# Attention block on one core: the product with v and the fp32 projections in two column halves, softmax sums by VectorE group adds, and the last output projection block by block

## The chip, the cores and the metric

One core of a Trainium2 chip runs one program. The metric is the device time of that program in microseconds (us). Engines are called by the profile's names: PE is TensorE (PEld its weight loads), DVE is VectorE, ACT is ScalarE, POOL is GpSimd, SP is SyncE.

## The reference

Input x is (4, 512, 48, 48) in fp32: 4 images, 512 channels, 2304 positions. 8 heads of 64 channels.

```python
hn = _group_norm(x, gn_scale, gn_bias)                       # 32 groups
qkv = einsum('oc,bchw->bohw', qkv_w, hn) + qkv_b             # fp32
q, k, v = qkv.reshape(b, 3, heads, 64, t).astype(float16)
w = softmax(einsum('bhct,bhcs->bhts', q * scale, k * scale))  # over s
a = einsum('bhts,bhcs->bhct', w, v).astype(float32)
return x + einsum('oc,bchw->bohw', proj_w, a) + proj_b
```

## The kernel before

The program is `fast_path`; the other path, `general_path`, runs only if a flag computed at the end of `fast_path` says that a softmax sum left its allowed range, and it does not run here. Heads are taken in pairs: a pair g (0 to 15) is two heads of one image, 128 channels; four pairs make an image. Positions stand in 18 key tiles of 128 and in 5 query blocks, four of 512 and one of 256.

**Attention.** The work of a pair is a list of 81 units (`units_of`): for a block of 512 queries one unit for each of the 18 key tiles, for the block of 256 one unit for two key tiles. `scores` (line 747) multiplies k and q of both heads, each on its own 64 rows of the array (line 755), into a PSUM tile of 128x1024, and ACT takes the exponential of that into fp16 (line 763). `values` (line 766) multiplies the exponentials with v, one product for each head (line 777). The stationary operand there has 65 columns: 64 of v and one of ones, so that row 64 of the result is the softmax sum. After a block's last unit `finish` (line 787) copies both results out of PSUM (line 792), sends the sums through small DMAs to take reciprocals across partitions (line 798) and to spread them again (line 804), and DVE multiplies (line 808).

**Projections.** q, k and v come from fp32 products of the normalised image with `wqkv`, accumulated over four channel chunks: `qk_items` (line 624, 40 items a pair, 32 of 512 columns and 8 of 256) and `v_items` (line 670, 72 items of 512 columns an image). An item is one product. Each fp32 product stands in the trace as two matmul records. `proj_items` (line 697) is the output projection of one block: 16 items, each with two fp32r products (high and low part of the weights, line 714); POOL first casts the four pairs' results to fp32r (line 704), and DVE adds bias and x (line 723).

**Order.** The main loop takes units two at a time, called a burst here: first the scores of this burst, then the values of the burst before, then `fill`, which issues as many items from the list `beside[g]` as the share of pair g's units that are done. There are 648 bursts, 40 or 41 a pair. A scheduler orders each engine's instructions when the program is built, so an instruction whose buffer isn't free lets later ones of its engine past. What `beside` holds: the q and k projections of a pair two pairs ahead, from pair 2 of an image the load and norm of the next image (`turn`) and then its v projection, in pair 3 of an image the q and k projections of the next image's first two pairs. The output projection of image b stands beside image b+1, in its pairs 0 and 1; that of image 2 stands in pairs 14 and 15, and that of image 3 after all attention:

```python
late = b == B - 1
beside[g + (2 + j // 3 if late else j // 4)] += proj_items(b - 1, j)
...
for j in range(NQ):
    for _, run in proj_items(B - 1, j):
        run()
```

The results of a pair (`atts[g]`) have 5 buffers, so pair 13 writes into the buffer that pair 8 had, which is free when image 2's output projection has read it. Ahead of the loop image 0 is normalised and its v and first two pairs of q and k are projected.

Of the kernel before, what the change touches and what calls it, by code (L numbers as in the profile page):

```python
# [30 lines left out]
SCALE = float(np.float16(1.0 / math.sqrt(math.sqrt(D))))  # L31
LAG = 2


# [431 lines left out]
def fast_path(  # L466
# [48 lines left out]
    nc.sync.dma_start(bproj, proj_b)  # L515
    brow = const.tile([1, C], F32, name="brow")
    nc.sync.dma_start(
# [41 lines left out]
    ones = const.tile([P, 1], F32, name="ones")  # L559
    nc.gpsimd.memset(ones, 1.0)  # L560

    bqk = const.tile([P, 2 * NC], F32, name="bqk")
# [47 lines left out]
    def qk_items(g):  # L610
# [8 lines left out]
        def one(part, j, c, pw):  # L619
            o, n = QBLOCKS[j]  # L620
            if c == 0:
                pw[0] = ps_w.tile([P, QB], F32, tag="pw", name=f"pqk_{g}_{part}_{j}")
            w0 = part * C + pr * P
            nc.tensor.matmul(  # L624
                pw[0][:, :n],
                wqkv[:, c, w0 : w0 + P],
                hn[b][c][:, o : o + n],
                start=(c == 0),
                stop=(c == NC - 1),
            )  # L630
# [27 lines left out]
    def v_items(b):  # L658
        items = []

        def new():
            for pr in range(NPAIR):
                t = vpool.tile([P, NT, 2, D + 1], F16, tag="v", name=f"v_{b}_{pr}")
                nc.gpsimd.memset(t[:, :, :, D : D + 1], 1.0)
                vv[b * NPAIR + pr] = t

        def one(i, c, pw):
            if c == 0:
                pw[0] = ps_w.tile([P, QB], F32, tag="pw", name=f"pv_{b}_{i}")
            nc.tensor.matmul(  # L670
                pw[0],
                hn[b][c][:, bass.ts(i, P)],
                wqkv[:, c, 2 * C :],
                start=(c == 0),
                stop=(c == NC - 1),
            )
            if c == NC - 1:
                for pr in range(NPAIR):
                    cols = bass.ts(pr, P)
                    nc.vector.tensor_tensor(  # L680
                        vv[b * NPAIR + pr][:, i, :, 0:D],
                        pw[0][:, cols].rearrange("p (h d) -> p h d", d=D),
                        bv[:, cols].rearrange("p (h d) -> p h d", d=D),
                        ALU.add,
                    )
# [50 lines left out]

    av, pts = {}, {}

    def units_of(g):
        found = []  # L740
        for j, (o, n) in enumerate(QBLOCKS):
            per = QB // n
            for i in range(0, NT, per):
                found.append((g, j, list(range(i, i + per))))
        return found

    def scores(u):
# [16 lines left out]
        pts[g, j, keys[0]] = pt  # L764

    def values(u):
        g, j, keys = u
        o, n = QBLOCKS[j]
        if keys[0] == 0:
            if j == 0:  # L770
                atts[g] = apool.tile([P, T], F16, tag="att", name=f"att_{g}")
            for h in range(2):
                av[h] = ps_av.tile([D + 1, QB], F32, tag=f"av{h}", name=f"av{h}_{g}_{j}")
        pt = pts.pop((g, j, keys[0]))
        for h in range(2):
            for a, i in enumerate(keys):
                nc.tensor.matmul(  # L777
                    av[h][:, :n],
                    vv[g][:, i, h, :],
                    pt[:, h, a * n : (a + 1) * n],  # L780
                    start=(i == 0),
                    stop=(i == NT - 1),
                )
        if keys[-1] == NT - 1:
            finish(g, j)

    def finish(g, j):
        o, n = QBLOCKS[j]
        per = n // P
        avx = work.tile([P, 2, QB], F32, tag="avx", name=f"avx_{g}_{j}")  # L790
        for h in range(2):
            nc.vector.tensor_copy(avx[0 : D + 1, h, :n], av[h][:, :n])  # L792
        first = 2 * o // P
        sm = sums[:, g, first : first + 2 * per].rearrange("p (h i) -> p h i", h=2)
        for h in range(2):
            nc.sync.dma_start(sm[:, h, :], avx[D : D + 1, h, :n])
        inv = small.tile([P, 2, QB // P], F32, tag="inv", name=f"inv_{g}_{j}")
# [4 lines left out]
        )  # L802
        ib = work.tile([D, 2, QB], F32, tag="ib", name=f"ib_{g}_{j}")
        nc.sync.dma_start(  # L804
            ib[:, :, :n], row[:, :n].unsqueeze(0).to_broadcast((D, 2, n))
        )
        for h in range(2):
            nc.vector.tensor_tensor(  # L808
                atts[g][h * D : (h + 1) * D, o : o + n],
                avx[0:D, h, :n],  # L810
                ib[:, h, :n],
                ALU.mult,
            )

    beside = {g: [] for g in range(NG)}
    for b in range(B):
        g = b * NPAIR  # L820
        for pr in (2, 3):
            beside[g + pr - 2] += qk_items(g + pr)
        if b > 0:
            for j in range(NQ):
                late = b == B - 1
                beside[g + (2 + j // 3 if late else j // 4)] += proj_items(b - 1, j)
        if b + 1 < B:

            def turn(b=b):
                hn[b + 1] = load_x(b + 1, (nc.gpsimd, nc.gpsimd))  # L830
                norm(b + 1)

            beside[g + 2].insert(0, (0.0, turn))
            vs = v_items(b + 1)
            beside[g + 2] += [(45.0, lambda: None)] + vs[:55]
            beside[g + 3] += vs[55:]
            for pr in (0, 1):
                beside[g + 3] += qk_items(g + NPAIR + pr)

# [7 lines left out]
    stream = [u for g in range(NG) for u in units_of(g)]  # L847
    last_of = {}
    for n, u in enumerate(stream):
        last_of[u[0]] = n  # L850
    per_pair = len(stream) // NG
    state = {"g": 0, "done": 0.0}

    def fill(n):

        g = stream[n][0]
        todo = beside[g]
        if state["g"] != g:
            state.update(g=g, done=0.0)
        if "total" not in state or state.get("of") != g:  # L860
            state.update(total=sum(w for w, _ in todo), of=g)
        place = n - g * per_pair + 1
        share = state["total"] * place / (per_pair - 2)
        while todo and state["done"] <= share:
            w, run = todo.pop(0)
            run()
            state["done"] += w

    waiting = []
    for n in range(0, len(stream), 2):  # L870
        burst = stream[n : n + 2]
        for u in burst:
            g = u[0]
            if g > 0 and u[1] == 0 and u[2][0] == 0:
                while beside[g - 1]:
# [6 lines left out]
    for u in waiting:  # L882
        values(u)
    for j in range(NQ):
        for _, run in proj_items(B - 1, j):
            run()


    flat = sums.rearrange("p g n -> p (g n)")
    low = small.tile([P, NG * 2 * NT], F32, tag="low", bufs=1, name="low")  # L890
    nc.vector.tensor_scalar(low, flat, SUM_MIN, None, ALU.is_ge)
    both = small.tile([P, NG * 2 * NT], F32, tag="both", bufs=1, name="both")
    nc.vector.scalar_tensor_tensor(both, flat, SUM_MAX, low, ALU.is_le, ALU.mult)
    good = small.tile([P, 1], F32, tag="good", bufs=1, name="good")
    nc.vector.tensor_reduce(good, both, AX.X, ALU.add)
    pf = ps_w.tile([1, 1], F32, tag="pw", name="count")
    nc.tensor.matmul(pf, good, ones, start=True, stop=True)
    nc.vector.tensor_scalar(flag, pf, float(B * HEADS * T) - 0.5, None, ALU.is_lt)
# [53 lines left out]
```

## Time and profile before

| | before |
|---|---|
| median of 3 runs | 2035.42 us (2035.2 to 2035.8) |
| the profiled execution | 2034.5 us, its span 2032.8 us |
| mean granted TensorE clock | 0.989 |
| busy share of the span | PE 96%, ACT 61%, DVE 26%, POOL 3% |

The span runs from the first to the last instruction of the profiled execution; 1.7 us of its time lie around the span. Busy is the time in which an engine has an instruction running. A matmul's record is longer than its place in the stream, since matmuls are pipelined: the distance between two starts is what one costs.

### The profile page before, as it was taken

Reading aid. Unit: us, or ns where it says so; the run is one execution under the profiler, and the core shown is the slowest. Engines: PE = TensorE matmul, PEld = TensorE weight load, DVE = VectorE, ACT = ScalarE, POOL = GpSimd, SP = SyncE. Lnnn points to the kernel's source line nnn. Section 1 sums busy time; section 2 is a strip of 40 time slices with the busy share of each in tenths; the row PEclk is TensorE's granted clock in tenths of the full one; section 3 lists DMA queues with packets and bytes.
Section 4 is the critical chain, followed back from the end, with each engine's and each line's share of the span. In section 5 each row is a group of like instructions: output and inputs, shape, how many; then the busy total and the mean of one; then the engine's idle time right before and its main releaser. Section 6 shows DMA issues by size and latency. Waiting matters only on the chain. (4 is left out here: it accounts for less than half of the span.)

```text
span 2032.8 us, 21633 instructions
## 1 busy us (share of the span) xinstructions
PE 1948.3 (96%) x8274; PEld 852.8 (42%) x8274; DVE 520.3 (26%) x1101; ACT 1243.3 (61%) x1297; POOL 66.1 (3%) x134
## 2 busy tenths in 40 slices
PE   3999999899999999899999999989999999999997
PEld 1444444234444553434344454433444434453335
DVE  5221222422222222522222222252222221131113
ACT  0007878755556667675555657775555788549990
POOL 0000000000000000100000010000000000010001
PEclk9999999899999999899999999989999999999999
DMA  5000002100000230400000041130000000141105
GB/s 191 0 0 6 16 9 87 31 11 9 11 6 14 76 101 11 135 11 11 8 6 14 6 130 53 49 98 11 9 6 11 14 11 14 42 137 22 27 24 176
DMA packets 83237, 81.80 MB, mean 40 GB/s; under 512 B 50356, under 2 KB 56500, under 8 KB 83124
## 3 DMA queue, kind: packets, MB, share of 16 engines
q1 hardware_dynamic: 77508, 60.67, 11.1%
q0 software_dynamic: 3456, 14.16, 1.8%
q10 hardware_dynamic: 2160, 5.51, 0.8%
q8 instruction: 67, 1.10, 0.2%
q14 instruction: 46, 0.38, 0.1%
HBM read 60.83 MB, written 19.17 MB: 39 GB/s over the span
## 5 line engine op out<-in xcount | busy, mean ns | idle before, releaser
L763 ACT ACTIVATE p<-ps 128x1024 f16<-128x1024 f32 x1296 | 1242.0, 1038 | 719.9 <-PE ps L755 668.7
L777 PE MATMUL av<-p,v 128*65 128x512 f16 (+1 forms) x2880 | 730.7, 368 | 25.9 <-DVE avx L792 25.9
L624 PE MATMUL pqk<-x,wqkv 128*128 128x512 f32 (+1 forms) x1280 | 556.1, 552 | 4.1 <-DVE x L598 4.1
L755 PE MATMUL ps<-q,k 64*128 64x512 f16 (+1 forms) x2880 | 435.5, 362 | 8.4 <-ACT p L763 6.0
L777 PEld LDWEIGHTS <-v 128*65 128x65 f16 x2880 | 262.9, 111 | 387.4 <-issue 294.6
L755 PEld LDWEIGHTS <-k 64*128 64x128 f16 x2880 | 125.3, 94 | 453.5 <-issue 448.9
L624 PEld LDWEIGHTS pqk<-x,wqkv 128*128 128x128 f32 x1280 | 241.6, 191 | 151.1 <-issue 98.9
L670 PE MATMUL pv<-wqkv,x 128*128 128x512 f32 x576 | 263.7, 593 | 0.0
L808 DVE TENSOR_TENSOR att<-avx,ib 64x512 f16<-64x512 f32 (+1 forms) x160 | 101.3, 633 | 295.2 <-DMA ib<-row 291.7
L670 PEld LDWEIGHTS pv<-wqkv,x 128*128 128x128 f32 x576 | 107.8, 190 | 102.6 <-issue 92.7
L792 DVE COPY avx<-av 65x512 f32<-65x512 f32 (+1 forms) x160 | 94.4, 628 | 214.2 <-PE av L777 213.0
L714 PE MATMUL pr<-a,whi 128*128 128x512 f32 (+1 forms) x320 | 131.5, 416 | 11.8 <-POOL a L704 7.1
L680 DVE TENSOR_TENSOR v<-pv,bv 128x128 f16<-128x128 f32 x288 | 63.8, 286 | 221.0 <-PE pv L670 220.9
L714 PE MATMUL pr<-a,wlo 128*128 128x512 f32 (+1 forms) x320 | 120.1, 380 | 0.0
L633 DVE TENSOR_SCALAR k<-pqk,bqk 128x512 f16<-128x512 f32 (+1 forms) x80 | 55.7, 696 | 247.3 <-PE pqk L624 247.1
L633 DVE TENSOR_SCALAR q<-pqk,bqk 128x512 f16<-128x512 f32 (+1 forms) x80 | 55.7, 696 | 237.6 <-PE pqk L624 237.3
L723 DVE SCALAR_TENSOR_TENSOR x<-pr,bproj,x 128x512 f32<-128x512 f32 (+1 forms) x80 | 55.5, 695 | 110.2 <-PE pr L714 80.8
L704 POOL CAST a<-att 128x512 fp32r<-128x512 f16 (+1 forms) x80 | 43.6, 582 | 1218.3 <-PE pr L714 553.9
L714 PEld LDWEIGHTS pr<-a,whi 128*128 128x128 f32 x320 | 61.2, 191 | 37.7 <-POOL a L704 18.8
L714 PEld LDWEIGHTS pr<-a,wlo 128*128 128x128 f32 x320 | 61.2, 191 | 11.0 <-issue 1.8
L798 DVE RECIPROCAL inv<-sums 128x8 f32<-128x8 f32 (+1 forms) x80 | 15.8, 197 | 149.2 <-DMA sums<-avx 146.9
L573 DVE BATCH_NORM_STATS2 st<-x 128x6 f32<-128x384 f32 x96 | 46.1, 537 | 8.7 <-DMA x<-x_dram 8.7
(36 smaller groups left out, 72.2 us busy)
## 6 DMA issues: line engine op xcount, KB each, us to landing
x<-x_dram SPq DMA_DIRECT2D x64, 256.0 KB, 2.9
ib<-row SPq DMA_DIRECT2D x64, 256.0 KB, 3.5
out_dram<-x SPq DMA_DIRECT2D x64, 256.0 KB, 2.4
x<-x_dram POOLq DMA_DIRECT2D x24, 576.0 KB, 7.1
wqkv<-qkv_wT_dram ACTq DMA_DIRECT2D x3, 1024.0 KB, 10.9
x<-x_dram SPq DMA_DIRECT2D x4, 576.0 KB, 7.6
x<-x_dram ACTq DMA_DIRECT2D x4, 576.0 KB, 9.0
sums<-avx SPq DMA_DIRECT2D x128, 2.0 KB, 2.0
```

The lines of the kernel that those rows point to most:

```text
L573: nc.vector.bn_stats(st[:, j, :], hn[b][c][:, bass.ts(j, SB)])
L624: nc.tensor.matmul(pw[0][:, :n], wqkv[:, c, w0 : w0 + P], hn[b][c][:, o : o + n], start=(c == 0), stop=(c == NC - 1),)
L633: nc.vector.tensor_scalar(qk[g][part][:, o : o + n], pw[0][:, :n], SCALE, bqk[:, col : col + 1], ALU.mult, ALU.add,)
L670: nc.tensor.matmul(pw[0], hn[b][c][:, bass.ts(i, P)], wqkv[:, c, 2 * C :], start=(c == 0), stop=(c == NC - 1),)
L680: nc.vector.tensor_tensor(vv[b * NPAIR + pr][:, i, :, 0:D], pw[0][:, cols].rearrange("p (h d) -> p h d", d=D), bv[:, cols].rearrange("p (h ...
L714: nc.tensor.matmul(pw[0][:, :n], w[:, c, bass.ts(m, P)], at[0][:, c, :n], start=(c == 0 and i == 0), stop=(c == NC - 1 and i == 1),)
L723: nc.vector.scalar_tensor_tensor(xt, pw[0][:, :n], bproj[:, m : m + 1], xt, ALU.add, ALU.add)
L755: nc.tensor.matmul(ps[:, h, a * n : (a + 1) * n], k[rows, bass.ts(i, P)], q[rows, o : o + n], start=True, stop=True,)
L763: nc.scalar.activation(pt, ps, AF.Exp)
L777: nc.tensor.matmul(av[h][:, :n], vv[g][:, i, h, :], pt[:, h, a * n : (a + 1) * n], start=(i == 0), stop=(i == NT - 1),)
L792: nc.vector.tensor_copy(avx[0 : D + 1, h, :n], av[h][:, :n])
L808: nc.vector.tensor_tensor(atts[g][h * D : (h + 1) * D, o : o + n], avx[0:D, h, :n], ib[:, h, :n], ALU.mult,)
```

## The change

`values` gives each head's product 64 columns of v instead of 65. Head 0 writes partitions 0 to 63 of one PSUM tile and head 1 partitions 64 to 127, so each uses one half of the array's columns, and the loops are turned so that the halves alternate. The column of ones goes away. Instead DVE adds the exponentials of up to six units of a block into an fp16 tile of 128x1024 (in `scores`, so one add for each unit but the first of a group), and one product with a 128x64 matrix of ones for each head and group gives the sums, again in two column halves, into a PSUM tile `sl`.

The fp32 projections of q, k and v are split likewise: each product with 128 output columns becomes two with 64. The output projection stays whole.

`finish` copies one 128x512 tile of results and one of sums, spreads the reciprocals with two DMAs instead of one, and the multiply is one instruction on POOL instead of two on DVE. v stands in one tile an image, and its bias is added by one DVE instruction a tile instead of four.

The order changes in the last six pairs: pair 11 no longer projects q and k of pair 13, which moves to pair 12 (and 14 to 13, 15 to 14). The output projection of image 2 stands beside pairs 12 (four blocks) and 13 (one block). That of image 3 stands beside pair 15, each block released 12 units after its attention ended; what is left over runs after the loop.

```diff
-    vpool = ctx.enter_context(tc.tile_pool(name="vpool", bufs=6))
+    vpool = ctx.enter_context(tc.tile_pool(name="vpool", bufs=2))
-    ppool = ctx.enter_context(tc.tile_pool(name="ppool", bufs=4))
+    ppool = ctx.enter_context(tc.tile_pool(name="ppool", bufs=6))
+    ps_l = ctx.enter_context(tc.tile_pool(name="ps_l", bufs=1, space=PSUM))
...
-            nc.tensor.matmul(
-                pw[0][:, :n],
-                wqkv[:, c, w0 : w0 + P],
-                hn[b][c][:, o : o + n],
+            for lo in (0, D):
+                nc.tensor.matmul(
+                    pw[0][lo : lo + D, :n],
+                    wqkv[:, c, w0 + lo : w0 + lo + D],
+                    hn[b][c][:, o : o + n],
...
-            nc.tensor.matmul(
-                pw[0],
-                hn[b][c][:, bass.ts(i, P)],
-                wqkv[:, c, 2 * C :],
+            for lo in (0, D):
+                nc.tensor.matmul(
+                    pw[0][lo : lo + D, :],
+                    hn[b][c][:, i * P + lo : i * P + lo + D],
+                    wqkv[:, c, 2 * C :],
...
-                for pr in range(NPAIR):
...
+                nc.vector.tensor_tensor(vv[b][:, i, :], pw[0], bv, ALU.add)
...
         nc.scalar.activation(pt, ps, AF.Exp)
         pts[g, j, keys[0]] = pt
 
+        m = keys[0] // len(keys)
+        key = (g, j, m // SUMMED)
+        if m % SUMMED == 0:
+            acc[key] = pt
+            return
+        before = acc[key]
+        if m % SUMMED == 1:
+            acc[key] = work.tile(
+                [P, 2, QB], F16, tag="acc", name=f"acc_{g}_{j}_{m // SUMMED}"
+            )
+        nc.vector.tensor_tensor(acc[key], before, pt, ALU.add)
...
-        for h in range(2):
-            for a, i in enumerate(keys):
+        for a, i in enumerate(keys):
+            for h in range(2):
+                lo = h * D
                 nc.tensor.matmul(
-                    av[h][:, :n],
-                    vv[g][:, i, h, :],
+                    av[0][lo : lo + D, :n],
+                    vv[b][:, i, pr * P + lo : pr * P + lo + D],
                     pt[:, h, a * n : (a + 1) * n],
...
+        if m % SUMMED == SUMMED - 1 or keys[-1] == NT - 1:
+            t = acc.pop((g, j, m // SUMMED))
+            for a in range(per):
+                for h in range(2):
+                    lo = h * D
+                    nc.tensor.matmul(
+                        sl[0][lo : lo + D, :n],
+                        ones16,
+                        t[:, h, a * n : (a + 1) * n],
...
-        for h in range(2):
-            nc.vector.tensor_copy(avx[0 : D + 1, h, :n], av[h][:, :n])
+        nc.vector.tensor_copy(avx[:, :n], av[0][:, :n])
+        slx = work.tile([P, QB], F32, tag="slx", bufs=1, name=f"slx_{g}_{j}")
+        nc.vector.tensor_copy(slx[:, :n], sl[0][:, :n])
...
+        for h in range(2):
+            nc.sync.dma_start(
+                ib[h * D : (h + 1) * D, :n], row[h : h + 1, :n].to_broadcast((D, n))
+            )
+        nc.gpsimd.tensor_tensor(
+            atts[g][:, o : o + n], avx[:, :n], ib[:, :n], ALU.mult
         )
-        for h in range(2):
-            nc.vector.tensor_tensor(
-                atts[g][h * D : (h + 1) * D, o : o + n],
...
+            put(g, qk_items(g + 2))
+            put(g + 1, qk_items(g + 3))
             vs = v_items(b + 1)
+            put(g + 2, [(0.0, turn), (45.0, lambda: None)] + vs[:55])
+            put(g + 3, vs[55:] + qk_items(g + 4))
+            if b + 2 < B:
+                put(g + 3, qk_items(g + 5))
+        else:
+            for pr in range(3):
+                put(g + pr, qk_items(g + pr + 1))
+        if b > 0:
+            for j in range(NQ):
+                put(g + j // 4, proj_items(b - 1, j))
+    ends = [i for i, u in enumerate(units_of(0)) if u[2][-1] == NT - 1]
+    for j in range(NQ):
+        put(NG - 1, proj_items(B - 1, j), ends[j] + 12)
...
+        share = total[g] * (place + 1) / (per_pair - 2)
+        while beside[g] and done[g] <= share and beside[g][0][2] <= place:
+            w, run, _ = beside[g].pop(0)
             run()
-            state["done"] += w
+            done[g] += w
...
-    for j in range(NQ):
-        for _, run in proj_items(B - 1, j):
-            run()
+    for _, run, _ in beside[NG - 1]:
+        run()
```

## Rows read from the trace of the kernel before

**Rows 1.** The page's first part: busy us, share of the span, instructions.

```profile
PE 1948.3 (96%) x8274; PEld 852.8 (42%) x8274; DVE 520.3 (26%) x1101; ACT 1243.3 (61%) x1297; POOL 66.1 (3%) x134
```

**Rows 2.** Stretches, one a pair: length, busy PE, PEld, DVE, ACT, POOL, clock, DMA.

```profile
159.20:254.40 95.20, 93.99 (x433) 39.39 (x432) 16.92 (x29) 77.82 (x82) 0.61 (x1) 1.00 0.05 12
...
351.40:478.50 127.10, 116.21 (x476) 45.47 (x475) 44.00 (x119) 77.12 (x83) 1.91 (x3) 0.96 0.10 33
478.50:617.60 139.10, 139.06 (x556) 58.81 (x555) 30.57 (x64) 78.44 (x83) 0.87 (x2) 1.00 0.04 9
617.60:742.20 124.60, 123.99 (x568) 61.61 (x568) 30.89 (x50) 78.69 (x83) 8.36 (x17) 1.00 0.25 69
742.20:845.00 102.80, 100.56 (x474) 45.09 (x473) 28.82 (x56) 78.45 (x83) 5.85 (x12) 0.98 0.21 68
...
1455.40:1594.40 139.00, 139.00 (x556) 58.73 (x555) 31.07 (x65) 78.35 (x82) 0.61 (x1) 1.00 0.04 9
1594.40:1689.80 95.40, 94.22 (x440) 40.08 (x440) 18.91 (x34) 78.10 (x83) 0.00 (x0) 1.00 0.07 13
1689.80:1829.30 139.50, 133.68 (x584) 65.48 (x582) 32.74 (x52) 77.49 (x82) 9.22 (x16) 0.99 0.23 68
1829.30:1903.90 74.60, 74.14 (x369) 26.53 (x368) 13.50 (x26) 74.49 (x82) 0.00 (x0) 1.00 0.09 20
1903.90:1979.80 75.90, 74.44 (x375) 27.33 (x374) 14.25 (x27) 74.73 (x82) 2.18 (x4) 1.00 0.11 24
1979.80:2032.80 53.00, 38.40 (x166) 27.82 (x164) 18.77 (x31) 0.06 (x1) 8.41 (x17) 0.92 0.57 178
```

**Rows 3.** Instructions in order of time in one burst: start, duration, engine, line.

```profile
303.81 0.60 PE L755 MATMUL ps<-q,k 64*128 64x512 f16 x4
...
304.34 1.05 PE L777 MATMUL av<-p,v 128*65 128x512 f16 x4
...
305.23 1.02 PE L624 MATMUL pqk<-x,wqkv 128*128 128x512 f32 x2
...
306.19 0.61 PE L755 MATMUL ps<-q,k 64*128 64x512 f16 x4
```

**Rows 4.** Groups of instructions by shape: count, busy us, mean ns, idle before.

```profile
L763 ACT ACTIVATE p<-ps 128x1024 f16<-128x1024 f32 x1296 | 1242.0, 1038 | 719.9 <-PE ps L755 668.7 <-PE av L777 49.3 <-ACT p L763 0.4
...
L624 PE MATMUL pqk<-x,wqkv 128*128 128x512 f32 x1024 | 495.3, 595 | 4.1 <-DVE x L598 4.1
```

**Rows 5.** ACT's instructions in order of time, 1756 to 1808 us.

```profile
1756.04 2.97 ACT L763 ACTIVATE p<-ps 128x1024 f16<-128x1024 f32 x3 [0.44 <-PE ps L755]
1807.29 1.02 ACT L763 ACTIVATE p<-ps 128x1024 f16<-128x1024 f32 x1 [48.28 <-PE av L777]
```

**Rows 6.** Groups of instructions by shape, DVE and POOL.

```profile
L808 DVE TENSOR_TENSOR att<-avx,ib 64x512 f16<-64x512 f32 x128 | 87.9, 687 | 241.8 <-DMA ib<-row 238.7 <-POOL a L704 1.3
L792 DVE COPY avx<-av 65x512 f32<-65x512 f32 x128 | 82.3, 682 | 199.2 <-PE av L777 198.2
...
L704 POOL CAST a<-att 128x512 fp32r<-128x512 f16 x64 | 37.0, 613 | 1177.8 <-PE pr L714 513.4 <-DVE att L808 468.6 <-issue 195.8
...
L808 DVE TENSOR_TENSOR att<-avx,ib 64x256 f16<-64x256 f32 x32 | 13.4, 417 | 53.3 <-DMA ib<-row 53.0
...
L539 DVE TENSOR_TENSOR wlo<-wproj,whi 128x512 fp32r<-128x512 f32 x4 | 2.7, 688 | 0.0
```

**Rows 7.** Who PE waited for: total us, times, longest.

```profile
PE av L777 <- DVE avx L792: 25.9, 9, 9.5
```

**Rows 8.** PE in order of time in that gap: two output projection items.

```profile
1767.18 0.39 PE L714 MATMUL pr<-a,whi 128*128 128x512 f32 x1
...
1767.64 0.39 PE L714 MATMUL pr<-a,whi 128*128 128x512 f32 x1
```

**Rows 9.** DMA issues: engine, count, KB each, us from issue to landing.

```profile
ib<-row SPq DMA_DIRECT2D x64, 256.0 KB, 3.5
...
sums<-avx SPq DMA_DIRECT2D x128, 2.0 KB, 2.0
```

More of the change, by code (lines that the diff above doesn't have):

```diff
@@ L32 @@
 LAG = 2
+SUMMED = 6
 GTB = 384
@@ L515, in fast_path @@
     nc.sync.dma_start(bproj, proj_b)
-    brow = const.tile([1, C], F32, name="brow")
+    brow = work.tile([1, C], F32, tag="avx", name="brow")
     nc.sync.dma_start(
@@ L669, in one @@
                 pw[0] = ps_w.tile([P, QB], F32, tag="pw", name=f"pv_{b}_{i}")
-            nc.tensor.matmul(
-                pw[0],
-                hn[b][c][:, bass.ts(i, P)],
-                wqkv[:, c, 2 * C :],
-                start=(c == 0),
-                stop=(c == NC - 1),
-            )
-            if c == NC - 1:
-                for pr in range(NPAIR):
-                    cols = bass.ts(pr, P)
-                    nc.vector.tensor_tensor(
[L681 to L685, printed above, removed]
+            for lo in (0, D):
[3 more added lines that the diff above has]
+                    wqkv[:, c, 2 * C :],
+                    start=(c == 0),
+                    stop=(c == NC - 1),
+                )
+            if c == NC - 1:
+                nc.vector.tensor_tensor(vv[b][:, i, :], pw[0], bv, ALU.add)
         items.append((0.0, new))
@@ L733, in proj_items @@
         return items
-    av, pts = {}, {}
+    av, sl, pts, acc = {}, {}, {}, {}
     def units_of(g):
@@ L742, in units_of @@
             per = QB // n
-            for i in range(0, NT, per):
-                found.append((g, j, list(range(i, i + per))))
+            units = [(g, j, list(range(i, i + per))) for i in range(0, NT, per)]
+            found += units
         return found
@@ L783, in values @@
                 )
+        per = len(keys)
+        m = keys[0] // per
+        if m % SUMMED == SUMMED - 1 or keys[-1] == NT - 1:
[7 more added lines that the diff above has]
+                        t[:, h, a * n : (a + 1) * n],
+                        start=(m < SUMMED and a == 0),
+                        stop=(keys[-1] == NT - 1 and a == per - 1),
+                    )
         if keys[-1] == NT - 1:
@@ L802, in finish, with put @@
         )
-        ib = work.tile([D, 2, QB], F32, tag="ib", name=f"ib_{g}_{j}")
-        nc.sync.dma_start(
-            ib[:, :, :n], row[:, :n].unsqueeze(0).to_broadcast((D, 2, n))
-        )
-        for h in range(2):
-            nc.vector.tensor_tensor(
-                atts[g][h * D : (h + 1) * D, o : o + n],
[L810 to L813, printed above, removed]
+        ib = work.tile([P, QB], F32, tag="ib", name=f"ib_{g}_{j}")
+        for h in range(2):
+            nc.sync.dma_start(
+                ib[h * D : (h + 1) * D, :n], row[h : h + 1, :n].to_broadcast((D, n))
+            )
+        nc.gpsimd.tensor_tensor(
+            atts[g][:, o : o + n], avx[:, :n], ib[:, :n], ALU.mult
+        )
     beside = {g: [] for g in range(NG)}
+    def put(g, items, after=0):
+        beside[g] += [(w, run, after) for w, run in items]
     for b in range(B):
         g = b * NPAIR
-        for pr in (2, 3):
-            beside[g + pr - 2] += qk_items(g + pr)
-        if b > 0:
-            for j in range(NQ):
-                late = b == B - 1
-                beside[g + (2 + j // 3 if late else j // 4)] += proj_items(b - 1, j)
         if b + 1 < B:
@@ L847, in fast_path @@
     stream = [u for g in range(NG) for u in units_of(g)]
-    last_of = {}
-    for n, u in enumerate(stream):
-        last_of[u[0]] = n
     per_pair = len(stream) // NG
-    state = {"g": 0, "done": 0.0}
+    total = {g: sum(w for w, _, _ in beside[g]) for g in range(NG)}
+    done = dict.fromkeys(range(NG), 0.0)
     def fill(n):
[L856 to L865, printed above, removed]
+        g, place = divmod(n, per_pair)
+        share = total[g] * (place + 1) / (per_pair - 2)
+        while beside[g] and done[g] <= share and beside[g][0][2] <= place:
+            w, run, _ = beside[g].pop(0)
             run()
-            state["done"] += w
+            done[g] += w
     waiting = []
@@ L873, in fast_path @@
             g = u[0]
-            if g > 0 and u[1] == 0 and u[2][0] == 0:
+            if g > 0:
                 while beside[g - 1]:
@@ L883, in fast_path @@
         values(u)
-    for j in range(NQ):
-        for _, run in proj_items(B - 1, j):
-            run()
[L889 to L895, printed above, removed]
+    for _, run, _ in beside[NG - 1]:
+        run()
+    good = small.tile([P, 2], F32, tag="good", bufs=1, name="good")
+    for i in range(2):
+        part = sums[:, bass.ts(i, NG // 2), :].rearrange("p g n -> p (g n)")
+        n = NG * NT
+        low = work.tile([P, n], F32, tag="avx", name=f"low_{i}")
+        nc.vector.tensor_scalar(low, part, SUM_MIN, None, ALU.is_ge)
+        both = work.tile([P, n], F32, tag="slx", bufs=1, name=f"both_{i}")
+        nc.vector.scalar_tensor_tensor(both, part, SUM_MAX, low, ALU.is_le, ALU.mult)
+        nc.vector.tensor_reduce(good[:, i : i + 1], both, AX.X, ALU.add)
     pf = ps_w.tile([1, 1], F32, tag="pw", name="count")
-    nc.tensor.matmul(pf, good, ones, start=True, stop=True)
+    for i in range(2):
+        nc.tensor.matmul(
+            pf, good[:, i : i + 1], ones, start=(i == 0), stop=(i == 1)
+        )
     nc.vector.tensor_scalar(flag, pf, float(B * HEADS * T) - 0.5, None, ALU.is_lt)
```

27 lines of the change are left out of this document (12 added, 15 removed).

## The prediction

> **What bounds the kernel now.** I read the page's busy times first: PE 96%, ACT 61%, DVE 26% [rows 1]. A mean over stages does not say which engine ends a stage, so next come stretches, one for each pair of heads [rows 2]. Pairs 0 to 13 take 95 to 140 us with PE busy almost throughout and ACT for some 78. Pairs 14 and 15 take 75 and 76 us with ACT full: 81 exponentials at 0.92 us. That is ACT's floor for a pair, 74.6. After pair 15 come 53 us without ACT. Pair 1 reads as pair 0 (97.0); pairs 6 and 10 (122.6, 124.3) as pair 2; pairs 7, 8 and 9 (139.1, 124.5, 99.9) as 3, 4 and 5.
>
> Next a single burst in order of time, by the distances of starts [rows 3]. Scores: 0.53 us for four products of 512 columns; they use 64 of the array's rows each and two run at once. Values: 0.89 for four, one after another, 0.22 each. Projection: 0.96 for one fp32 item of two records, with the switch back to scores. Without the switch I take 0.85 an item. Pairs 0 and 3 agree: pair 3 has 17 items of v and 40 of q and k more, 53 at full width, and takes 43.9 us more, 0.83 each. So of pair 0's 95.2 us its 40 items (36 at full width) are 30.6 and attention 64.6. ACT waits for scores through 669 us of the run [rows 4]. PE is the bound, except where a burst has no items.
>
> One place stands out. In pair 13 ACT waits 48.3 us [rows 5] while PE works off the rest of its projections and the whole output projection of image 2, which the text puts into pairs 14 and 15. Pair 13 waits for the buffer that this projection must release. PE is not idle in that stretch of 139.5 us [rows 2]; the loss is that pairs 14 and 15 then run at ACT's pace with nothing beside.
>
> **The change part by part.**
>
> *Values in column halves.* The trace has no products in column halves; it has row halves, and these run two at once [rows 3]. The cost lies between 0.45 us a burst (as the row halves) and 0.89 (no overlap, nothing gained). I take 0.45: 0.445 saved a burst, 40.5 bursts, 18.0 us a pair.
>
> *Sums.* PE gets 32 products with ones a pair, 24 of 512 and 8 of 256 columns, in halves two at a time: 14 places of 0.22, 3.1 us. Net 14.9 us a pair where PE is the bound.
>
> *DVE adds.* 14 of 81 units start a group, so 67 adds of 1024 fp16 elements a pair. No such row exists. A two-input fp32 row of 512 elements, as many bytes, takes 688 ns; the rows of 256 and 512 elements differ by 270 ns, 1.05 ns an element [rows 6], so by elements it would be 1.23 us. I take 0.69, as the operands have just that row's bytes: 46 us a pair, beside 17 to 44 us that DVE has now, less 6.3 for the multiplies that leave [rows 1, 2, 6]. That is 57 us in pair 0 and at most 84 in pair 2, inside the stretches, so PE hides it. Without that cover (1.23 us) it is a rival below. The Trainium skill, page "VectorE: DVE Perf Modes", section "Mode 2×_1P — pack two bf16 into one 32-bit read", lets a 16-bit two-input operation make two results a cycle; by its 0.96 GHz I estimate 0.53 us and a fixed part for an add, and the sum would be the same. No row here shows that mode.
>
> *fp32 projections in column halves.* Four records an item instead of two, each with half the columns of the array. From both sides: 0.85 an item if the halves overlap, 1.70 if not; no row excludes either. I take 0.85, since the only halves in the trace do overlap. Nothing gained, nothing lost.
>
> *v and finish.* One bias add instead of four, one copy more of sums, one DMA more on SP, the multiply on POOL (some 0.6 us as its cast [rows 6], at most two of them): beside PE, nothing. What waits behind them: PE's next values wait for the copy of `av`. That wait is 25.9 us now, in 9 pieces of up to 9.5 [rows 7]; I leave it as it is. New is that a copy can find an add ahead of it, 0.69 us. I allow it at one in four of the 80 finishes: +14 us. The range has 0 and 55 for it.
>
> *Pairs 0 to 10.* 14.9 us off each, but for three kinds: pairs 2, 6 and 10 save only in the 22 bursts that have v items, 8.1 (in the others ACT sets the pace); pairs 3 and 7 all; pairs 4 and 8 have some 23 bursts with output projection, which stays whole, so a switch more of 0.1: 12.9. Sum: 14.9 × 6 + 8.1 × 3 + 12.9 × 2 = 139.5.
>
> *Pairs 11 to 15.* Pair 11 loses 40 items: 139.0 − 30.6 − 14.9 = 93.5. Pair 12 becomes like pair 8, 111.6; pair 13 like pair 9, 85.0; pair 14 like pair 0, 80.3. Pair 15 has ACT's 74.6, and three blocks of output projection that `fill` issues 16 items at a time: 0.46 an item [rows 8] is 7.4 us, of which ACT has two exponentials ready, 1.84; 5.5 lost, three times: 91. Together 461.4 where there were 524.4: 63.0 saved.
>
> *Tail.* 53 us now for five blocks. Left are two: the last finish, two copies of 0.68, three DMA legs of 2 to 3.5 [rows 6, 9] and their issue, some 11 us beside which block 3 is projected; then casts, 16 items of half width and the last store, 16. I take 27: 26 saved.
>
> Sum: 139.5 + 63.0 + 26 − 14 = 214.5. The profiled execution's 2034.5 becomes 1820. That execution stands 0.9 below the median, which is nothing here.
>
> **The rivals.**
>
> *Halves take turns, fp32 runs pay a pass.* The two records of an item's first half use the same columns, so the second waits for the first, 0.43 us. If records start only in their order, the other half starts with that second record, and a run of fp32 records ends one pass later than it would in full overlap. For it: in the burst read, the records start in the order of the program [rows 3]. Against: nothing. By `fill`'s weights 463 of the 648 bursts have fp32 items (36 or 37 in a pair with 40 items, 22 with v, 39 in pairs 3, 7 and 11). At 0.40 that is +185: 2005. The Trainium skill, page "TensorE: Matmul & The Clock Gate", section "The mechanism", states this order, strict in start and end; by it this rival would hold. Chance 0.24.
>
> *fp32 halves do not overlap.* The other side. All 864 full-width items (576 for q and k, 288 for v) cost 0.85 more: +734, 2554. It decides from 0.25 us an item on, when the 214 are used up. For it: the trace has no fp32 in halves of any kind. Against: the row halves. Slower with chance 0.14.
>
> *DVE becomes the bound.* Adds of 1.23 us are 82 a pair: 93 in pair 0, 104 in pairs 5 and 13. Against the times above that lengthens pairs 0, 1, 5, 9, 11, 13, 14 and 15 and little else, by some 110: 1930. Chance 0.07.
>
> *The values' halves don't overlap either*: then the change adds instead of saving; with the second rival, over 2850. Chance 0.02.
>
> **How the numbers follow.** Forecast 0.53, at 1820 with a range of its own from 1785 (no copy found behind an add, pair 15 without its lost time) to 1875 (all copies found behind one). The range of all: from 1785 to 2035, which takes in DVE as the bound and the paid pass, and leaves out the fp32 halves without overlap and a little on either side. What a measurement here can tell is about 0.2%, 4 us. Faster: the forecast, DVE, and most of the first rival (its 185 would have to be 214): 0.53 + 0.07 + 0.17 = 0.77. Same 0.03. Slower: 0.04 of the first rival, 0.14, 0.02 = 0.20.
>
> **What would show it.** Right: in a burst four values start within 0.45 us; an item's four fp32 records take 0.85; the adds' mean is near 0.69 us; DVE is busy some 1150 us and PE less long than now; no gap of tens of us in pair 13; ACT's last exponential 27 us before the end. Wrong: an item's records at 1.28 or 1.70; DVE full in single-item pairs; PE waiting for `avx` much more than 26 us; ACT idle many us in pair 15.

## The result and the profile after

The changed kernel takes 1921.41 us (median; 1919.6 to 1922.2). The kernel before, on the same chip, took 2035.31. The ratio is 0.9442, with a 95% interval from 0.9426 to 0.9459. That is faster, and inside the range, but 114 us were saved where the sum said 214.5. The experiments look for the missing 101.

The page's first part after the change, against [rows 1]:

```profile
PE 1816.3 (95%) x10644; PEld 656.0 (34%) x10644; DVE 1141.3 (60%) x1800; ACT 1259.2 (66%) x1297; POOL 174.7 (9%) x199
```

DVE's 1141 us stand close to the 1150 forecast. PE is busy for less time, but still through 95% of the span. So PE remains the bound, and the question is what it does.

The stretches by pair, columns as in [rows 2]:

```profile
160.10:262.20 102.10, 97.90 (x546) 31.08 (x546) 58.87 (x89) 79.36 (x81) 5.22 (x4) 1.00 0.04 10
262.20:356.80 94.60, 91.56 (x553) 30.38 (x550) 62.56 (x95) 78.83 (x82) 10.82 (x12) 0.99 0.13 41
356.80:477.50 120.70, 108.22 (x618) 35.14 (x620) 77.92 (x133) 78.32 (x81) 10.16 (x10) 0.93 0.12 30
477.50:606.20 128.70, 128.47 (x783) 43.07 (x780) 69.06 (x108) 78.50 (x83) 5.48 (x5) 1.00 0.05 10
606.20:721.90 115.70, 114.77 (x683) 48.81 (x684) 71.07 (x108) 78.50 (x82) 15.79 (x18) 1.00 0.25 76
721.90:813.40 91.50, 89.54 (x585) 33.25 (x582) 63.63 (x99) 78.54 (x82) 13.82 (x19) 1.00 0.22 72
...
1385.80:1487.20 101.40, 100.25 (x623) 33.51 (x620) 64.49 (x97) 78.43 (x83) 6.18 (x5) 1.00 0.05 10
1487.20:1603.00 115.80, 114.84 (x683) 48.86 (x684) 71.87 (x108) 78.58 (x83) 14.74 (x17) 1.00 0.27 77
1603.00:1693.20 90.20, 89.31 (x585) 33.25 (x582) 62.13 (x97) 78.45 (x83) 9.82 (x11) 1.00 0.11 26
1693.20:1793.00 99.80, 95.88 (x553) 30.93 (x552) 60.76 (x92) 79.28 (x83) 7.26 (x6) 1.00 0.10 24
1793.00:1889.60 96.60, 93.58 (x495) 38.05 (x495) 61.77 (x94) 78.21 (x82) 14.22 (x17) 1.00 0.26 76
1889.60:1917.70 28.10, 15.30 (x69) 10.84 (x67) 8.88 (x19) 0.00 (x0) 4.21 (x7) 0.78 0.38 102
```

These are pairs 0 to 5, pairs 11 to 15 and the tail. The forecast had 80.3 for pair 0 and for pair 14. They take 102.1 and 99.8, which are the two largest misses. Pair 0 was 95.2 before [rows 2], so there the change made a stretch longer. Pair 1 comes next, with 94.6 where 97.0 less 14.9 was forecast. Pairs 2 to 5 lie 2 to 5 us above their forecast (119, 124.2, 111.7, 87.9). Pair 11 is 8 above, pairs 12, 13 and 15 are 4 to 6 above, and the tail is 1 above. The gap of 48 us in pair 13 [rows 5] is gone; ACT's longest waits there are now 1.00 us, this one among them:

```profile
1666.71 3.89 ACT L759 ACTIVATE p<-ps 128x1024 f16<-128x1024 f32 x4 [1.00 <-PE ps L751]
```

So the three large misses are in pairs that have one fp32 item to a burst and nothing else beside attention. Here is pair 0 in order of time on PE, as in [rows 3]. First a place where the two column halves of an item stand together, then the pattern of 28 of the 50 runs of fp32 records in that pair:

```profile
210.11 0.38 PE L751 MATMUL ps<-q,k 64*128 64x512 f16 x2
210.42 0.62 PE L787 MATMUL av<-p,v 128*64 128x512 f16 x4
210.88 1.02 PE L629 MATMUL pqk<-x,wqkv 128*64 128x512 f32 x4
211.84 0.39 PE L751 MATMUL ps<-q,k 64*128 64x512 f16 x2
...
223.43 0.39 PE L751 MATMUL ps<-q,k 64*128 64x512 f16 x2
223.75 0.41 PE L787 MATMUL av<-p,v 128*64 128x512 f16 x2
223.99 1.02 PE L629 MATMUL pqk<-x,wqkv 128*64 128x512 f32 x2
224.95 0.39 PE L751 MATMUL ps<-q,k 64*128 64x512 f16 x2
225.27 0.41 PE L787 MATMUL av<-p,v 128*64 128x512 f16 x2
225.51 1.02 PE L629 MATMUL pqk<-x,wqkv 128*64 128x512 f32 x2
226.46 0.39 PE L751 MATMUL ps<-q,k 64*128 64x512 f16 x2
```

The count at the end of the fp32 rows is what to read. Four records, both halves of an item, take 1.02 us from 210.88. Two records, one half, take the same 1.02 from 223.99. A half that stands alone uses half of the array and costs as much as both. The program's text issues the two halves one right after the other. The order in which PE gets them is fixed when the kernel is built, and it has put one half behind the values of one unit and the other half behind the values of the next.

The groups that answer to [rows 4] and [rows 6], and the adds:

```profile
L759 ACT ACTIVATE p<-ps 128x1024 f16<-128x1024 f32 x1296 | 1257.9, 1022 | 612.7 <-PE ps L751 583.5 <-DVE acc L772 20.2 <-DVE x L719 3.0
L772 DVE TENSOR_TENSOR acc<-acc,p 128x1024 f16<-128x1024 f16 x848 | 617.3, 729 | 318.8 <-ACT p L759 305.8 <-DVE inv L823 0.2
L629 PE MATMUL pqk<-x,wqkv 128*64 128x512 f32 x2048 | 557.0, 595 | 3.9 <-DVE x L602 3.9
L772 DVE TENSOR_TENSOR acc<-p,p 128x1024 f16<-128x1024 f16 x224 | 157.2, 702 | 165.1 <-ACT p L759 163.9
L833 POOL TENSOR_TENSOR att<-avx,ib 128x512 f16<-128x512 f32 x64 | 86.6, 1353 | 1382.1 <-DMA ib<-row 1184.3 <-DVE acc L772 163.3 <-DVE q L638 23.5
L815 DVE COPY avx<-av 128x512 f32<-128x512 f32 x64 | 44.2, 691 | 49.1 <-PE av L787 49.1
```

And who PE waited for, against [rows 7]. The last line is from the kernel before:

```profile
PE gmean L580 <- DVE mv L578: 41.5, 4, 26.3
PE sl L801 <- DVE acc L772: 20.9, 19, 3.8
PE ps L751 <- ACT p L759: 7.1, 34, 0.5
...
PE av L787 <- DVE avx L815: 2.2, 3, 1.0
...
PE gmean L576 <- DVE mv L574: 25.1, 1, 25.1
```

The wait for `avx` fell from 25.9 to 2.2. A new wait of 20.9 stands beside it: the product with ones waits for its last add. A third one is for `gmean`, a small product in the norm of an image. One piece of it, 26.3 us and 25.1 before, lies ahead of the loop; the other 15.2 us are new and lie in pairs 2, 6 and 10, where VectorE normalises the next image beside the adds. In pairs 2 and 10 the wait for `avx` had its longest pieces before (9.5 and 5.8). So in the loop PE waits 38.3 us for VectorE at these three places, where it waited 25.9. ACT has a new wait as well, 20.2 us, which the releases put down to a probability buffer that an add still reads.

The DMAs of the sums took 2.0 us as before [rows 9]. Those for `ib`, twice as many and half as large, took 3.0 where 3.5 was:

```profile
ib<-row SPq DMA_DIRECT2D x128, 128.0 KB, 3.0
...
sums<-slx SPq DMA_DIRECT2D x128, 2.0 KB, 2.0
```

To weigh these things, each kernel's PE records were sorted by their starts. Three sums come out of each trace. **Idle halves**: half of the time in which exactly one column half works, with 0.43 us for a record of 512 fp32 columns and 0.21 for one of 512 fp16 columns. **Changes**: how often neighbouring products differ between row halves, column halves and the whole array; each is put at 0.095 us, the mean by which starts at a change are further apart. **Rest**: what is left of the span when busy time and changes are taken off, mostly waits.

| kernel | span | idle halves | changes (us) | rest |
|---|---|---|---|---|
| before | 2032.8 | 0 | 1650 (157) | 181 |
| changed | 1917.7 | 76.5 | 1742 (166) | 203 |
| fp32_whole | 1943.3 | 15.1 | 2260 (215) | 241 |
| pe_in_order | 1926.0 | 12.6 | 1380 (131) | 312 |
| no_adds | 1897.0 | 72.4 | 1738 (165) | 188 |
| order_alone | 2012.1 | 0 | 1554 (148) | 174 |
| halves_glued | 1855.1 | 13.7 | 1719 (163) | 206 |
| glued_spread | 1850.3 | 12.6 | 1687 (160) | 205 |
| fp32_halves_alone | 2130.2 | 37.0 | 2166 (206) | 192 |
| glued_no_adds | 1837.3 | 13.5 | 1736 (165) | 187 |
| fp32_halves_alone_glued | 2099.3 | 8.4 | 2135 (203) | 193 |

### The profile page after: what moved, and what is told of

It reads as the page before. It is cut to its first block, busy times and chain, and to the rows that moved or that the text cites. A ratio compares the mean times of both kernels' runs of the same rounds, so it can differ in the third digit from the quotient of the medians.

```text
span 1917.7 us, 27997 instructions
## 1 busy us (share of the span) xinstructions
PE 1816.3 (95%) x10644; PEld 656.0 (34%) x10644; DVE 1141.3 (60%) x1800; ACT 1259.2 (66%) x1297; POOL 174.7 (9%) x199
## 4 chain that ended last, share of the span: by engine, by line
PE 78%; DMA 6%; ACT 5%; DVE 5%; issue 4%; POOL 1%; SPq 0%; ACTq 0%; DVEq 0%; POOLq 0%
PE pqk L629 26%; PE ps L751 16%; PE av L787 15%; PE pv L673 12%; PE pr L710 7%; ACT p L759 5%; PE sl L801 3%; DVE acc L772 3%; DMA x<-x_dram 2%; DMA out_dram<-x 1%; DMA sums<-slx 1%; DMA row<-inv 1%; DVE st L577 1%; DMA wqkv<-qkv_wT_dram 1%; DMA ib<-row 1%
## 5 line engine op out<-in xcount | busy, mean ns | idle before, releaser
L772 DVE TENSOR_TENSOR acc<-acc,p 128x1024 f16<-128x1024 f16 x848 | 617.3, 729 | 318.8 <-ACT p L759 305.8
L629 PE MATMUL pqk<-x,wqkv 128*64 128x512 f32 (+1 forms) x2560 | 621.4, 552 | 3.9 <-DVE x L602 3.9
L787 PE MATMUL av<-p,v 128*64 128x512 f16 (+1 forms) x2880 | 464.3, 374 | 2.2 <-DVE avx L815 2.2
L673 PE MATMUL pv<-wqkv,x 128*64 128x512 f32 x1152 | 278.3, 593 | 0.0
L629 PEld LDWEIGHTS pqk<-x,wqkv 128*64 128x64 f32 x2560 | 198.7, 137 | 190.1 <-issue 109.6
L772 DVE TENSOR_TENSOR acc<-p,p 128x1024 f16<-128x1024 f16 x224 | 157.2, 702 | 165.1 <-ACT p L759 163.9
L833 POOL TENSOR_TENSOR att<-avx,ib 128x512 f16<-128x512 f32 (+1 forms) x80 | 100.5, 1257 | 1537.0 <-DMA ib<-row 1302.1
L787 PEld LDWEIGHTS <-v 128*64 128x64 f16 x2880 | 128.9, 108 | 247.7 <-issue 241.8
L673 PEld LDWEIGHTS pv<-wqkv,x 128*64 128x64 f32 x1152 | 84.8, 137 | 114.6 <-issue 94.1
L801 PE MATMUL sl<-acc,ones 128*64 128x512 f16 (+1 forms) x512 | 95.7, 362 | 21.4 <-DVE acc L772 20.9
L719 DVE SCALAR_TENSOR_TENSOR x<-pr,bproj,x 128x512 f32<-128x512 f32 (+1 forms) x80 | 55.3, 694 | 35.0 <-PE pr L710 22.6
```

The costliest lines, as they stand in the source:

```text
L629: nc.tensor.matmul(pw[0][lo : lo + D, :n], wqkv[:, c, w0 + lo : w0 + lo + D], hn[b][c][:, o : o + n], start=(c == 0), stop=(c == NC - 1),)
L673: nc.tensor.matmul(pw[0][lo : lo + D, :], hn[b][c][:, i * P + lo : i * P + lo + D], wqkv[:, c, 2 * C :], start=(c == 0), stop=(c == NC - 1),)
L719: nc.vector.scalar_tensor_tensor(xt, pw[0][:, :n], bproj[:, m : m + 1], xt, ALU.add, ALU.add)
L772: nc.vector.tensor_tensor(acc[key], before, pt, ALU.add)
L787: nc.tensor.matmul(av[0][lo : lo + D, :n], vv[b][:, i, pr * P + lo : pr * P + lo + D], pt[:, h, a * n : (a + 1) * n], start=(i == 0), stop ...
L801: nc.tensor.matmul(sl[0][lo : lo + D, :n], ones16, t[:, h, a * n : (a + 1) * n], start=(m < SUMMED and a == 0), stop=(keys[-1] == NT - 1 a ...
```

## The experiments

Theory A: the order fixed at build time parts the halves, and PE loses the 76 us. Its rivals: the missing time is the adds and the waits that they bring (B), or halved fp32 products are dear in themselves (C).

**fp32_whole**: the changed kernel with q, k and v projected at full width again.

```diff
-            for lo in (0, D):
-                nc.tensor.matmul(
-                    pw[0][lo : lo + D, :n],
-                    wqkv[:, c, w0 + lo : w0 + lo + D],
+            nc.tensor.matmul(
+                pw[0][:, :n],
+                wqkv[:, c, w0 : w0 + P],
...
```

> The changed kernel, but the fp32 products of q, k and v at full width (128 columns) again; values and sums stay in halves. In the trace of the changed kernel, lone halves leave half of the array's columns idle for 76 us in sum, most of it beside fp32 records. Theory A (the instruction order, fixed when the program is built, parts the two halves of an item; halves that stand together do overlap): most of the 76 us goes, some 65, and each run of fp32 items costs one more switch of tiling, 0.1 us, some 460 times, so about 1900 us (1880 to 1920). Theory B (the adds on DVE hold everything up; the order does not matter): only the switches are new, about 1965 us. Theory C (the two halves of an fp32 item cannot run at once without paying a pass at the end of a run): the passes go, -185, and the switches come, about 1780 us.

Measured: 1942.19 us, ratio 0.955 (0.9521 to 0.9579). C falls: without the fp32 halves the kernel is slower, not 140 us faster. The time lies between A's 1880 to 1920 and B's 1965, so by the letter neither holds. The loss that A speaks of does go (idle halves 61 us less), but 518 more changes, 49 us, and 38 us more of rest take more than that. Whole fp32 products next to halved values cost a change of mode that halved ones don't; what the 38 us are, the last section shows.

**pe_in_order**: each product on PE, from the projections on, is held behind the one before it in the order of the text, with no wait on any other engine.

```diff
+    def pin(ins):
+        if "pe" in last:
+            tc.add_manual_dep(
+                ins.ins,
+                last["pe"].name,
...
+        last["pe"] = ins.ins
...
-                nc.tensor.matmul(
+                pin(nc.tensor.matmul(
...
```

> The changed kernel, with PE's matmuls from the projections on held in the order in which the program text issues them (ordering edges only, no new wait on a result; the matmuls of the norm are left free). Theory A: both halves of each item stand together, the idle half columns fall from 76 us to under 20 and the switches from 1742 to about 1450, so 1921 - 60 - 25 = about 1840 us (1815 to 1865). Theory B: the same adds are waited for, now as open waits of PE for the products with ones, and nothing is gained: 1905 us or more.

Measured: 1931.37, ratio 0.9498 (0.9482 to 0.9514). By the letter A fails here and B's 1905 or more holds. The trace says why:

```profile
PE ps L765 <- ACT p L773: 45.6, 104, 0.5
PE sl L815 <- DVE acc L786: 40.1, 27, 5.1
PE av L801 <- DVE avx L829: 26.9, 39, 2.6
```

The halves stand together (idle halves 12.6), and these three waits are 82 us longer than in the changed kernel. The text's order is better than the built one in the halves and in the changes (362 fewer, 34 us) and worse in the waits, so this run moved several things at once and doesn't decide.

**no_adds**: the adds are left out, and the product with ones takes only the last unit of each group, so the sums are partial.

```diff
...
-        nc.vector.tensor_tensor(acc[key], before, pt, ALU.add)
+        acc[key] = pt
```

> The changed kernel without DVE's adds: the product with ones takes only the last unit of each group, so the softmax sums are partial (the allowed range of the sums is widened so that the other path stays off). 1072 instructions and 775 us of DVE's busy time go. Theory A: PE's waits for the adds go (21 us as the trace shows them), and what is left hangs on whether the order still parts halves: between 1870 and 1915 us, with the idle half columns read from its trace telling which. Theory B: the whole shortfall of 100 us against the forecast comes back: 1830 us or less.

Measured: 1898.14, ratio 0.9334 (0.9318 to 0.935). The adds cost 23 us, not the 91 or more that B needs, and the idle halves stay at 72.

**order_alone**: the kernel before with nothing but the new places of the projections (the change's `put`, `total` and `done`).

```diff
-            beside[g + 2] += [(45.0, lambda: None)] + vs[:55]
+            put(g + 2, [(0.0, turn), (45.0, lambda: None)] + vs[:55])
...
+        put(NG - 1, proj_items(B - 1, j), ends[j] + 12)
```

> The kernel before with nothing but the new places of the items: projections of pairs 13 to 15 one pair ahead, output projection of image 2 beside pairs 12 and 13, that of image 3 beside pair 15. By the terms of the forecast without the halves, pairs 11 to 15 take 108 + 124 + 100 + 95 + 92 = 519 us instead of 524, and the tail 27 instead of 53: about 2004 us (1990 to 2015). If the order alone were worth the 63 + 26 us that the forecast booked in these stretches: 1946 us.

Measured: 2012.78, ratio 0.9898 (0.9881 to 0.9914). The new places are worth 21 us by themselves (the kernel before took 2034.0 beside it); the forecast's own steps give 2004 for them.

**halves_glued**: the changed kernel, and only the second half of each fp32 item and of each product with values is held behind its first half and given priority. All else stays as the build orders it.

```diff
-            for lo in (0, D):
-                nc.tensor.matmul(
+            halves = []
+            for lo in (0, D):
+                with tc.high_priority() if lo else nullcontext():
+                    ins = nc.tensor.matmul(
...
+                halves.append(ins)
+            glue(*halves)
...
```

> The changed kernel, with the second half of each fp32 item and of each product with v ordered right behind its first half when the program is built (an ordering edge and a high priority); all else is free to move, unlike in the run with PE in program order. Theory A (parted halves): the idle half columns fall from 76 us to under 15, and the waits stay as they are, since nothing else is held: 1921 - 62 = about 1860 us (1840 to 1880), pair 0 from 102 to some 88 us. Theory D (PE would have had to wait for exponentials and adds in that time anyway, as the run in program order suggests): the halves stand together and the time goes to waits instead, 1905 us or more.

Measured: 1857.1, ratio 0.912 (0.9105 to 0.9135). A holds to within 3 us. Pairs 0 and 14, and pair 0 in order of time:

```profile
158.80:246.70 87.90, 84.97 (x546) 27.61 (x546) 59.65 (x89) 77.97 (x82) 4.97 (x4) 1.00 0.04 10
...
1641.90:1729.70 87.80, 84.72 (x553) 28.00 (x552) 60.79 (x92) 78.15 (x83) 7.92 (x6) 1.00 0.11 25
```

```profile
205.27 0.41 PE L823 MATMUL sl<-acc,ones 128*64 128x512 f16 x2 [0.33 <-DVE acc L790]
205.48 1.05 PE L641 MATMUL pqk<-x,wqkv 128*64 128x512 f32 x4
206.47 0.60 PE L769 MATMUL ps<-q,k 64*128 64x512 f16 x4
207.00 0.62 PE L807 MATMUL av<-p,v 128*64 128x512 f16 x4
207.46 1.02 PE L641 MATMUL pqk<-x,wqkv 128*64 128x512 f32 x4
```

The rows of fp32 now count four. The number of changes is much as before the hold (1719 against 1742), and the rest too (206 against 203), so the 64 us are the idle halves: 62.8 of them went.

**glued_spread**: besides, the last output projections of pair 15 are released one item to a unit.

```diff
-        put(NG - 1, proj_items(B - 1, j), ends[j] + 12)
+        for i, item in enumerate(proj_items(B - 1, j)):
+            put(NG - 1, [item], ends[j] + 12 + i)
```

> As halves_glued, and in pair 15 the items of the last output projection released one by one, an item a unit, instead of 16 at once. The forecast put the cost of the lumps at 3 x 5.5 us: so 10 to 16 us below halves_glued, pair 15 from some 96 to 80 to 87 us. If the lumps cost nothing because the order puts scores between them: the same time as halves_glued.

Measured: 1852.83, ratio 0.9095 (0.9078 to 0.9113), the quickest of the versions that leave nothing out. 4 us came, less than the 10 to 16 expected: pair 15 went from 96.6 to 88.9, and the span of all else grew by 3.

**glued_no_adds**: the hold, with the adds left out as in no_adds.

> Halves held together, and besides VectorE's adds left out (the product with ones takes only the last unit of each group, so the sums are partial). Theory A plus adds: parted halves and the adds are two separate costs, so the adds cost here what they cost beside parted halves, 2013 - 1990 in other words the 23 us between the changed kernel (1921.4) and the one without adds (1898.1): 1857 - 23 = 1834, within 1826 to 1842; that leaves 14 us to the forecast of 1820. Rival E: the adds were hidden behind time that parted halves lost, or the other way round, and only one of the two can be gained: 1850 or more where the adds no longer matter, 1820 or less where they matter more once PE is quicker.

Measured: 1842.77, ratio 0.9059 (0.9044 to 0.9074). That is 14 us by the medians and 12 by the ratios, between the two expectations and just outside the first. Without the adds PE's wait for `avx` is back, 16.1 where halves_glued has 2.0 for `avx` and 18.9 for the adds:

```profile
PE av L799 <- DVE avx L829: 16.1, 5, 5.1
```

So these two waits stand largely in each other's place. With the wait for `gmean` in the loop (14.0 in halves_glued, 6.5 here) PE waits 34.9 us for VectorE with the adds and 22.6 without, and the 12 us between them are most of what the adds cost here. Why they cost 23 beside parted halves stays open.

**fp32_halves_alone**: the kernel before with only the fp32 projections in column halves; values stay whole.

```diff
+            for lo in (0, D):
+                nc.tensor.matmul(
+                    pw[0][lo : lo + D, :n],
+                    wqkv[:, c, w0 + lo : w0 + lo + D],
...
```

> The kernel before with only the fp32 products of q, k and v in column halves; product with v in 65 columns, sums and order as before. Theory A: halves overlap, so the items cost what they did, and each run of items behind a product with v now costs a switch of tiling, 0.1 us some 460 times, plus what the order parts: 2080 us (2060 to 2120), an item's four records within 0.86 us. Theory C (a pass paid at each run's end): 2034 + 185 + 46 = 2265 us.

Measured: 2132.87, ratio 1.048 (1.0462 to 1.0497). By themselves the halves make the kernel slower, by 96 us, 13 more than A's range allows. C's 2265 is far off.

**fp32_halves_alone_glued**: the same, with the two halves held together.

> The kernel before with only the fp32 projections of q, k and v in column halves, and the second half of each held behind the first; values stay whole. Theory A, parted halves: the 97 us that the halves alone cost without that hold were 37 of idle half columns, some 49 for 516 more changes between modes of the array, and waits. Held together the 37 go, and of the changes those stay that lie between whole values and halved items, some 400 at 0.1: 2035 + 45 = 2080, within 2060 to 2095. If halves were free in themselves and only their parting cost anything: 2025 to 2045. Rival F, halves that stand together cost something of their own that the accounting does not see: 2110 or more.

Measured: 2104.03, ratio 1.0352 (1.0324 to 1.038). It lies between the ranges of A and F. The hold takes 29 us of idle halves off, and 26 come by the ratios. Over the kernel before stay 71, of which 8 are idle halves. The other 63 stand beside 485 more changes, which at 0.095 us are 46. The 17 that are left are what F supposed, but not a price of the halves' own: an fp32 item directly behind a change takes longer, and a whole one more so than a halved one (last section).

## Why the prediction was right, and where it missed

*The number.* That the kernel gets faster was right, and so was the mechanism that the gain was to come from. But 1921 lies 46 us above the forecast's own range, 1785 to 1875. It lies in the range of all only because that reached up to 2035 for DVE as the bound (1930) and for the paid pass (2005), and neither came. That the time stands close to 1930 is luck. The forecast's own ends were also set too wide: by its terms they are 1820 − 14 − 16.5 = 1789.5 and 1820 − 14 + 55 = 1861, and 14.9 less 23 switches of 0.1 is 12.6, not 12.9 (pairs 4 and 8). With the halves held together the kernel takes 1857, inside that range.

*Values in column halves: right.* In the burst at 210.42 the four values take 0.46 us to the next product, where 0.45 was forecast and 0.89 was the time before [rows 3]. *fp32 in column halves: right in mechanism.* Both halves take 0.96 from 210.88 to the next scores with its change, as the whole item did [rows 3]. The two rivals that made the fp32 halves dear fall with it. The paid pass rested on an order by records. The single records at 210.88 start at 0, 3, 429 and 432 ns, so the other half's first record doesn't wait for the first half's second (which record belongs to which half is read from their order). The Trainium skill, page "TensorE: Matmul & The Clock Gate", section "The mechanism", has products strict in their order of start and end; the trace agrees if a product's two records count as one, and the rival had counted them singly.

*Nothing gained, nothing lost, the 14.9 us a pair: this is where the sum missed.* The sum took the halves as standing together wherever the text writes them together. The built order parts them, and 64 us of the missing 101 are that; halves_glued shows it. In pair 0 idle halves are 13.8 us, in pair 14 12.0, in pair 1 8.2, in the others 1 to 5. Pairs 5, 9 and 13 have one fp32 item to a burst too, besides one block of output projection, and lose only 3 to 4. Why the build parts the halves where it does was not tried.

*The adds: the size nearly right, the place wrong.* They take 0.70 and 0.73 us, and 0.69 was taken; DVE is not the bound (1898 without adds, against 1921). The forecast left the wait for `avx` at 25.9 and booked 14 us more for copies of `av` that find an add ahead, 39.9 together. The wait for `avx` fell to 2.2 instead; PE waits 20.9 for the last add of a group and 15.2 for the norm, 38.3 together. That the sum comes out is luck, since the forecast had neither place. ACT waits 20.2 through buffers. In all the adds cost 12 to 23 us, depending on the halves.

*Order and tail: right, 9 us too much.* order_alone came to 2012.8 for a forecast of 2004. The tail is 28.1 for 27. In pair 15 ACT waits for pieces of output projection, as forecast, but the pair takes 96.6 where 91 was forecast:

```profile
1850.70 1.94 ACT L759 ACTIVATE p<-ps 128x1024 f16<-128x1024 f32 x2 [1.19 <-PE ps L751]
1855.72 3.97 ACT L759 ACTIVATE p<-ps 128x1024 f16<-128x1024 f32 x4 [3.09 <-PE ps L751]
```

*The multiply on POOL: wrong, without a price.* 0.6 us was taken and 1.35 measured, but no wait of PE is put down to it, and POOL is busy 9%.

*The balance.* 101 = 64 for parted halves + 9 for the order + about 28 that no experiment separates; the adds' 14 were in the forecast. For the 28: halves_glued still has 13.7 us of idle halves, and it has 165 more changes than order_alone, 16 us at 0.095, of which the forecast had some 6 (the switches in pairs 4, 8 and 12). In pair 0 the changes are 122 for 92 before. The clock adds a little. In pair 2, where PE waits 10.4 us for the norm, the granted clock is 0.93, and it was 0.96 before [rows 2]; over the whole span PE was busy for 39 us at the lower of its two levels (1.2 GHz), for 31 before, which I estimate at some 4 us. This split is argued from the sums, not shown.

## What to carry to other kernels

Two half-array products are worth a gain only while they stand side by side in the order that the engine gets. Read that order from the trace by the counts of records in a burst, and hold the second half behind the first if the build may move it; here that took a few lines and was worth 64 us. Pinning the whole order instead cost more in waits here than it brought. A product that fills the whole array gains nothing in itself from halving: the fp32 items here take 0.86 us either way. Their halving pays only because their neighbours are halved too and changes of mode go away (1942 us whole, 1921 halved, 1857 held together); beside whole values it cost 71 to 96 us.

## What the runs showed that was not expected

A change of the array's mode costs the same in every run. Where neighbouring products differ in mode, their starts are mostly 0.09 to 0.10 us further apart than within a mode, with column halves as in the kernel before. The Trainium skill, page "TensorEngine Tiling (Array Packing)", section "Key Properties", says that changing the tiling mode drains the engine; the trace agrees as far as each change costs this time.

An fp32 item directly behind a change costs more on top. The first three lines are from fp32_whole, where whole items stand behind halved values, the others from fp32_halves_alone_glued, where halved items stand behind whole values:

```profile
206.50 1.13 PE L628 MATMUL pqk<-x,wqkv 128*128 128x512 f32 x2
207.56 0.67 PE L749 MATMUL ps<-q,k 64*128 64x512 f16 x4
L628 PE MATMUL pqk<-x,wqkv 128*128 128x512 f32 x1024 | 531.8, 628 | 4.5 <-DVE x L602 4.5
...
239.84 1.08 PE L637 MATMUL pqk<-x,wqkv 128*64 128x512 f32 x4
240.85 0.60 PE L775 MATMUL ps<-q,k 64*128 64x512 f16 x4
L637 PE MATMUL pqk<-x,wqkv 128*64 128x512 f32 x2048 | 512.5, 610 | 4.0 <-DVE x L598 4.0
```

To the next scores the whole item takes 1.06 us and the halved one 1.01, where 0.96 is the time behind a product of the same mode [rows 3]. The first record of such an item lasts 697 or 643 ns where the others last 592, and the second record starts that much later. The mean record shows it: 628 and 610 ns for the 595 of the kernels before and after. In fp32_whole this makes 39 us (33 ns for 1024 records of 512 columns, 22 for 256 of 256 columns), which is the 38 us of rest; in fp32_halves_alone_glued, with 15 and 9 ns, some 18, beside the 17 us that were left over there.

An fp32 product in column halves shows no loss against the whole one when both halves run behind a product of the same mode: 0.86 us for 512 columns, with record starts at 0, 3, 429 and 432 ns. One half alone takes the same 0.86.

POOL's two-input multiply of 128x512 takes 1353 ns, 2.2 times the cast of the same size in the kernel before [rows 6].
